# A one-core attention and gated-FFN kernel: stacks moved in halves, even head groups first, the weight comparison on Pool and ScalarE, and unread TensorE passes in the start and in the seam

## The chip, the core and the metric

The kernel runs on one core of a Trainium2 chip. The metric is the device time of one execution in microseconds (us). A core has five engines that run their own instruction streams and wait for each other through semaphores: TensorE (PE; its weight loads are shown apart as PEld), VectorE (DVE), ScalarE (ACT), GpSimd (POOL) and SyncE (SP), which here only issues DMA transfers. ACT issues some transfers too; while it does, it computes nothing.

## The reference

Input x has 32 sequences of 256 tokens with 128 features, in fp32. One layer is computed:

```python
Q, K, V = split_heads(x @ Wq.T + bq), ...          # 16 heads of 8
scores = Q K^T / sqrt(8);  causal mask;  scores -= (i - j)
attn   = softmax(scores);  out = attn V
x = layernorm(x + out @ Wo.T + bo)
h = silu((x @ w1.T) * s1) * ((x @ w2.T) * s2)       # 128 -> 512
h = gelu((h @ h1.T) * sh1);  h = gelu((h @ h2.T) * sh2)   # 512 -> 512
x = layernorm(x + (h @ w3.T) * s3)
```

The FFN weights are small integers times a factor. The kernel looks at run time whether all of them survive a rounding to the matmul's fp32r form without loss; if so, it runs a branch in which each FFN product takes two passes (a rounded part and the rest of the activations), else one with plain fp32. With the inputs here the first branch runs.

## The kernel before

**Pairs.** Two sequences (512 tokens) make a pair; there are 16, numbered n. `project(n)` loads x, turns it over on PE, and makes q and k as 128 x 512 (`pq`, `pk`); ACT adds the bias and rounds (`qhi`, `khi`), DVE takes the rest (`qlo`, `klo`).

**Stacks.** The scores of a head are one matmul of 62 to 64 rows: rounded and rest parts of 8 features, position terms, the mask, and for the second use the maxima. `fill` writes the position rows of the tiles `qs[n % 2]` and `ks[n % 2]` (128 x 8 x 512), and `stack(n, ...)` (L305) moves the q and k parts into them by DMA: for q, and for k, four transfers of 256 KB, 16 target partitions by 8 groups of heads by 512 tokens. A head group g (0 to 7) is one slice of those tiles. q goes on SP's queue; k goes on ACT's queue for pairs 0, 1 and 2 and on SP's later.

**Maxima, then weights.** `row_maxima(n, i)`, i = 0 to 11, computes scores with queries on partitions, in one of three PSUM tiles of two banks (`two`), adds the mask by four small bf16 matmuls (`mask`), and DVE reduces them to maxima (`m`). Of each three, two handle one group each and the third the diagonal blocks of both groups. `maxima_to_rows` turns maxima over on PE (`pm`), ACT copies (`mhi`), DVE takes the rest (`mlo`), and SP moves both into the last rows of `qs`. For pair 0 that is done in two parts, groups 0 to 3 and 4 to 7. `weigh(n, i)` then computes the scores the other way round, with the maxima subtracted in the matmul; ACT takes Exp (`e`), POOL zeroes what the mask hides. `outputs` multiplies by the values (`pa`), and turns the result over (`pt`); `finish` applies Wo (`pon`, `po`).

**Order.** The wrapper `InOrder` keeps PE, DVE, ACT and SP in the order in which the code is written. That order sets all: an engine that waits holds everything behind it. `step(n)` runs the twelve weights of pair n between the twelve maxima of pair n + 1, and between them the projection of pair n + 2 and ends of earlier pairs; then it stacks pair n + 2; then the FFN of pair n - 1 (`feed`) runs with the rest of the attention of pair n (`rest`). Maxima run `LEAD` = 2 places ahead in step 0 and `LAG` = 3 behind in step 1. Step 0 has no FFN, so the way from its last weights through `rest` to step 1 is called the seam. Between step 0 and step 1 each engine reads a number and branches.

**Before step 0** (L684 to L720): projections of pairs 0 and 1 with their fills and stacks, the twelve maxima of pair 0, the load of the FFN layers (2.9 MB, SP), and the first two maxima of pair 1.

**The comparison.** `inexact_weights` (L622) goes through 11 blocks of 128 x 512 weights, one between two score blocks of step 0. ACT rounds a block (`w_near`, `h_near`), DVE compares it with the whole and adds up the differences (`differ`); at the end PE adds over partitions (`pcount`), DVE makes a number of it.

**Waits of transfers.** The built program gives transfers eight completion semaphores in turn, and a transfer waits, on the engine that issues it, until the last one that used its semaphore has landed.

Of the kernel before, what the change touches and what calls it, by code (L numbers as in the profile page):

```python
# [17 lines left out]
P = 128  # L18
# [43 lines left out]
def tile_attn_ffn(  # L62
# [49 lines left out]
    ks = [const.tile([P, W, TOK], F32R, name=f"ks{i}") for i in range(2)]  # L112
    sctx = ctx.enter_context(ExitStack())
# [20 lines left out]

    wq_sb = const.tile([P, D], F32, name="wq_sb")
# [10 lines left out]
    for src, w_bias, bias, nm, eng in (  # L146
        (wqT, bq_sb, bq, "q", act), (wkT, bk_sb, bk, "k", sp),
    ):
        raw = setup.tile([P, D], F32, name=f"raw{nm}")
        eng.dma_start(out=raw, in_=src)  # L150
        raws.append(raw)
        for p in range(2):

            eng.dma_start(
                out=w_bias[64 * p : 64 * p + 64, :],
                in_=bias.rearrange("(f p) d e -> p d e f", p=2)[p],
            )
# [7 lines left out]
    for raw, dst, scale in zip(raws, (wq_sb, wk_sb), (HD**-0.5, 1.0)):  # L165
        act.activation(
            dst.rearrange("i (p d g) -> i p d g", p=2, g=W),
            raw.rearrange("i (g p d) -> i p d g", p=2, g=W), AF.Copy, scale=scale,
        )
    act.activation(bq_sb, bq_sb, AF.Copy, scale=HD**-0.5)  # L170
# [41 lines left out]
    fill(ks[0], "k", act)  # L212

# [13 lines left out]
    for i in range(2):  # L227
# [10 lines left out]
        ("w1", w1T, 1, HID), ("w2", w2T, 1, HID), ("h1", h1T, KC, HID), ("h2", h2T, KC, HID),  # L238
        ("w3", w3T, KC, D),
# [9 lines left out]
    def load_layers(pool):  # L249
        got = {}  # L250
        for nm, src, k, o in layers:
            got[nm] = pool.tile([P, k, o], F32, name=f"{nm}_sb")
            sp.dma_start(out=got[nm], in_=src.rearrange("(k p) o -> p k o", p=P))
        return got
# [40 lines left out]
    def halves(n, ps, bias, nm):  # L295
        pool = setup if n == 1 else hlp
        hi = pool.tile([P, TOK], F32R, name=f"{nm}hi_{n}", tag=f"{nm}hi")
        act.activation(hi, ps, AF.Identity, bias=bias)
        lo = pool.tile([P, TOK], F32R, name=f"{nm}lo_{n}", tag=f"{nm}lo")
        vec.scalar_tensor_tensor(  # L300
            lo, ps, bias, hi.bitcast(F32), ALU.add, ALU.subtract
        )
        return hi, lo

    def stack(n, nm, eng=sp):  # L305
        for r, part in {
            "q": ((0, 0), (1, 0), (2, 1), (3, 1)), "k": ((0, 0), (2, 0), (1, 1), (3, 1))
        }[nm]:
            eng.dma_start(
                out=pairs[n][nm][PAIRING + r :: W, :, :].bitcast(F32),  # L310
                in_=pairs[n][nm + "s"][part].bitcast(F32),
            )
# [309 lines left out]
    def inexact_weights():  # L622

        found = const.tile([P, 11], F32, name="found")
        at = 0
        for nm, *_ in layers:
            rows = [t[nm].rearrange("p k o -> p (k o)") for t in (loaded, near)]
            for c in range(0, rows[0].shape[1], HID):
                whole, part = (t[:, c : c + HID] for t in rows)
                act.copy(part, whole)  # L630
                differ = once.tile([P, HID], F32, name=f"differ_{at}", tag="differ")
                vec.scalar_tensor_tensor(
                    differ, whole, 1.0, part.bitcast(F32), ALU.mult, ALU.not_equal,
                    accum_out=found[:, at : at + 1],
                )
                at += 1
                yield
        ones_col = const.tile([P, 1], F32, name="ones_col")
        nc.gpsimd.memset(ones_col, 1.0)
        count = work("pcount")  # L640
# [41 lines left out]


# [6 lines left out]
    stack(0, "k", act)  # L690
    fill(ks[1], "k", act)
# [3 lines left out]
    run(ahead)  # L695
    stack(1, "q", sp)
    stack(1, "k", act)
    project_values(0)
    for a in range(G):
        act.dma_start(  # L700
            out=wo_sb[C * HD * a : C * HD * (a + 1), :],
            in_=woT[:, :, a, :].rearrange("c d o -> (c d) o"),
        )
    sctx.close()
    ep = enter(tc.tile_pool(name="ep", bufs=5))
    op = enter(tc.tile_pool(name="op", bufs=2))
    yp = enter(tc.tile_pool(name="yp", bufs=2))
    lctx = ctx.enter_context(ExitStack())
    once = lctx.enter_context(tc.tile_pool(name="once", bufs=1))
    for i in range(6):  # L710
        row_maxima(0, i)
    project_values(1)
    maxima_to_rows(0, (0,))
    loaded = load_layers(once)
    for i in range(6, 3 * G):
        row_maxima(0, i)
    maxima_to_rows(0, (1,))
# [7 lines left out]
    def step(n, exact=None, ws=None, hp=None, gp=None):  # L725
# [4 lines left out]
            last(n - 2, exact, ws, gp) if n > 1 else first_norm(0) if n else inexact_weights()  # L730
        )
        ahead = project(n + 2) if n + 2 < NPAIR else iter(())
        for i in range(3 * G):
            weigh(n, i)
            j = i + {0: LEAD, 1: -LAG}.get(n, 0)
# [11 lines left out]
            if i in ((0, 2) if n > 1 else (0, 2, 4, 6)) if n else i < 11:  # L747
                next(settling, None)
# [10 lines left out]
        if n + 2 < NPAIR:  # L759
            stack(n + 2, "q")  # L760
            stack(n + 2, "k", sp if n else act)


        def rest():
            for _ in range(3):
                next(side)
                yield
# [12 lines left out]
            next(last_steps)  # L780
            yield
# [102 lines left out]
```

## Time and profile before

| | us |
|---|---|
| median of three runs (822.67 to 824.28) | 822.67 |
| profiled execution, whole time | 824.84 |
| its span | 822.9 |
| PE busy in the span | 781.9 |
| DVE busy | 635.9 |
| ACT busy | 527.7 |
| POOL busy | 260.6 |

The span is what the profile covers, from the first instruction to the last; all times below count from its start. A busy PE is not PE at its peak: the ends of its pipelined matmuls are modelled, and its clock is granted by a throttle (0.968 of full in the mean here, 1.00 in the body). The busy share is a mean over stages with different limits: 15 steps of the body are alike, and the start, step 0 and the seam are not. In the groups, all instructions of the ordered engines have line 58, that of the wrapper, so they are told apart by their tiles.

### The profile page before, as it was taken

Reading aid. Unit: us, or ns where it says so; the run is one execution under the profiler, and the core shown is the slowest. Engines: PE = TensorE matmul, PEld = TensorE weight load, DVE = VectorE, ACT = ScalarE, POOL = GpSimd, SP = SyncE. Lnnn points to the kernel's source line nnn. Section 1 sums busy time; section 2 is a strip of 40 time slices with the busy share of each in tenths; the row PEclk is TensorE's granted clock in tenths of the full one; section 3 lists DMA queues with packets and bytes.
Section 4 is the critical chain, followed back from the end, with each engine's and each line's share of the span. In section 5 each row is a group of like instructions: output and inputs, shape, how many; then the busy total and the mean of one; then the engine's idle time right before and its main releaser. Section 6 shows DMA issues by size and latency. Waiting matters only on the chain.

```text
span 822.9 us, 17420 instructions
## 1 busy us (share of the span) xinstructions
PE 781.9 (95%) x7046; PEld 554.9 (67%) x7046; DVE 635.9 (77%) x1247; ACT 527.7 (64%) x719; POOL 260.6 (32%) x341
## 2 busy tenths in 40 slices
PE   4897999999999999999999999999999999999995
PEld 1664576676767677676767767676766767666673
DVE  6786777878788887888878887888888788873674
ACT  5055556667676776666576676657666676758673
POOL 5032413323142332414242341424233232424211
PEclk8569999999999999999999999999999999999997
DMA  6824040402304040320404041140404023000001
GB/s 148 209 63 108 14 106 14 105 16 60 73 14 106 27 107 14 81 53 14 106 27 106 14 104 29 36 97 15 107 26 104 4 57 64 14 5 14 0 3 41
DMA packets 39898, 47.49 MB, mean 58 GB/s; under 512 B 3968, under 2 KB 21632, under 8 KB 39808
## 3 DMA queue, kind: packets, MB, share of 16 engines
q1 hardware_dynamic: 37152, 42.82, 21.8%
q10 hardware_dynamic: 2656, 3.48, 1.9%
q8 instruction: 57, 0.93, 0.5%
q14 instruction: 33, 0.27, 0.1%
HBM read 7.48 MB, written 4.19 MB: 14 GB/s over the span
## 4 chain that ended last, share of the span: by engine, by line
PE 80%; ACT 5%; DVE 3%; issue 1%; DMA 1%; SPq 0%; POOL 0%; ACTq 0%; POOLq 0%; DVEq 0%
PE peven L58 14%; PE podd L58 14%; PE pa L58 11%; PE pw L58 10%; PE s L58 10%; PE s_2d L58 2%; PE s_3d L58 2%; PE s_1d L58 2%; PE po L58 2%; ACT e L58 2%; PE pt L58 2%; PE pk L58 2%; PE pv L58 2%; PE s_0d L58 1%; PE pq L58 1%; ACT yT L58 1%
## 5 line engine op out<-in xcount | busy, mean ns | idle before, releaser
L58 DVE TENSOR_REDUCE m<-s 128x4 f32<-128x1024 f32 x128 | 155.6, 1218 | 11.0 <-PE s L58 9.4
L58 ACT ACTIVATE e<-s 128x1024 f32<-128x1024 f32 x128 | 130.6, 1021 | 44.9 <-PE s L58 30.6
L463 POOL TENSOR_SCALAR_AFFINE_SELECT e<-e 128x512 f32<-128x512 f32 x128 | 83.1, 650 | 221.5 <-ACT e L58 192.2
L58 PE MATMUL podd<-h,h_near 128*128 128x512 f32 x512 | 131.4, 403 | 0.9 <-DVE m L58 0.5
L58 PE MATMUL peven<-hodd,h_near 128*128 128x512 f32 x512 | 122.7, 396 | 0.0
L58 PEld LDWEIGHTS peven<-hodd,h_near 128*128 128x128 f32 x512 | 95.7, 187 | 23.4 <-DVE hodd L58 0.3
L58 PEld LDWEIGHTS podd<-h,h_near 128*128 128x128 f32 x512 | 91.7, 188 | 23.1 <-DVE h L58 3.5
L58 ACT ACTIVATE hodd<-podd,sh 128x512 fp32r<-128x512 f32 x64 | 44.1, 688 | 62.8 <-PE podd L58 62.6
L58 PE MATMUL pw<-x1T,w_near 128*128 128x512 f32 x256 | 75.6, 418 | 1.1 <-DVE h0w L58 1.1
L58 PEld LDWEIGHTS s<-qs,ks 64*128 64x128 f32 x512 | 39.1, 189 | 51.9 <-DVE m L58 17.9
L58 PE MATMUL pa<-e,vaug 128*32 128x256 f32 x1024 | 72.2, 397 | 0.0
L274 POOL TENSOR_TENSOR rsa<-rsa,half 128x4 f32<-128x4 f32 x16 | 16.3, 1018 | 175.9 <-DVE rsa L58 175.9
L58 DVE SCALAR_TENSOR_TENSOR h0w<-pw,s,sg 128x512 f32<-128x512 f32 x64 | 47.9, 748 | 30.3 <-ACT sg L58 30.3
L58 PE MATMUL s<-qs,ks 64*128 64x256 f32 x512 | 65.6, 336 | 1.0 <-ACT e L58 0.5
L58 DVE TENSOR_TENSOR heven<-evenw,heven 128x512 fp32r<-128x512 f32 x64 | 44.2, 692 | 26.6 <-ACT evenw L58 26.1
L58 ACT ACT_TABLE_LOAD x47 | 60.3, 1283 | 3.5 <-issue 2.6
L58 ACT ACTIVATE sg<-pw,s 128x512 f32<-128x512 f32 x64 | 43.7, 684 | 28.2 <-PE pw L58 27.8
L58 ACT ACTIVATE heven<-peven,sh 128x512 fp32r<-128x512 f32 x48 | 33.4, 696 | 39.8 <-PE peven L58 39.8
L58 PE MATMUL s<-ks,qs 62*128 62x256 f32 x512 | 55.8, 297 | 2.6 <-ACT e_0d L58 2.1
L58 PEld LDWEIGHTS pw<-x1T,w_near 128*128 128x128 f32 x256 | 43.4, 188 | 18.4 <-ACT nothing L58 5.8
L581 POOL TENSOR_TENSOR h<-h0w,h 128x512 fp32r<-128x512 f32 x31 | 40.0, 1291 | 43.5 <-DVE h L58 41.2
L58 DVE TENSOR_TENSOR hodd<-oddw,hodd 128x512 fp32r<-128x512 f32 x64 | 43.7, 684 | 10.0 <-ACT oddw L58 9.8
(147 smaller groups left out, 1415.7 us busy)
## 6 DMA issues: line engine op xcount, KB each, us to landing
qs<-qhi SPq DMA_DIRECT2D x32, 256.0 KB
qs<-qlo SPq DMA_DIRECT2D x32, 256.0 KB
ks<-khi SPq DMA_DIRECT2D x26, 256.0 KB
ks<-klo SPq DMA_DIRECT2D x26, 256.0 KB
x<-in_x_dram SPq DMA_DIRECT2D x16, 256.0 KB
out_dram<-z SPq DMA_DIRECT2D x15, 256.0 KB
ks<-khi ACTq DMA_DIRECT2D x6, 256.0 KB
ks<-klo ACTq DMA_DIRECT2D x6, 256.0 KB
```

The costliest lines, as they stand in the source:

```text
L58: return lambda *args, **kw: self.tc.keep_in_program_order(call(*args, **kw))
L274: nc.gpsimd.tensor_tensor(rs, rs, half[:, 0:NT], ALU.pow)
L463: nc.gpsimd.affine_select(out=on_diagonal, in_=on_diagonal, pattern=[[0, on_diagonal.shape[1]], [1, P]], base=0, channel_multiplier=-1, co ...
L581: (nc.gpsimd if o < (1 if final else 2) else vec).tensor_tensor(h[:, 1, o, :], whole, h[:, 0, o, :].bitcast(F32), ALU.subtract)
```

## The change

1. `stack` moves each part in two halves: the order of the weights' columns is changed so that 64 source partitions hold the even groups and 64 the odd ones, and the transfers of the even groups come first. 16 transfers of 128 KB take the place of 8 of 256 KB, for each pair. For pairs 1 and 2, k moves from ACT's queue to SP's.
2. Maxima of pair 0 run in the order 0, 3, 6, 9 (even groups), 1, 2, 4, 5, then 7, 8, 10, 11. DVE's `qlo` and `klo` of pair 1 (`due`) come after the first two.
3. The FFN layers are loaded right after the stacks of pair 0, w3 before h1 and h2; the pools that the FFN and outputs use are made earlier, and no longer share memory with the set-up.
4. The comparison runs before step 0: ACT rounds, POOL subtracts, ACT takes the absolute value with a sum, one block behind. The last sum is in place 5 of step 0 and the count in place 8. DVE's part is gone but for one small compare.
5. `warm` issues passes of 512 bf16 columns whose result nobody reads: 4 ahead of the first maxima, 1 behind each of the last four, 4 before the second `maxima_to_rows`, and in `rest` of step 0 four times 4: 28 in all.
6. Smaller: the biases are loaded by SP in one transfer each; the scaling of `bq` is behind the first key fill; Wo is loaded by SP; the value products of pairs 0 and 1 come after the eighth maxima.

```diff
+    lctx = ctx.enter_context(ExitStack())
+    once = lctx.enter_context(tc.tile_pool(name="once", bufs=1))
     sctx = ctx.enter_context(ExitStack())
...
+    for w_bias, bias in ((bq_sb, bq), (bk_sb, bk)):
+        sp.dma_start(out=w_bias, in_=bias.rearrange("c d (e o) -> (c d e) o", o=1))
...
     fill(ks[0], "k", act)
+    act.activation(bq_sb, bq_sb, AF.Copy, scale=HD**-0.5)
...
-        vec.scalar_tensor_tensor(
-            lo, ps, bias, hi.bitcast(F32), ALU.add, ALU.subtract
+        due.append(
+            lambda: vec.scalar_tensor_tensor(lo, ps, bias, hi.bitcast(F32), ALU.add, ALU.subtract)
         )
+        if n != 1:
+            run_due()
...
     def stack(n, nm, eng=sp):
-        for r, part in {
-            "q": ((0, 0), (1, 0), (2, 1), (3, 1)), "k": ((0, 0), (2, 0), (1, 1), (3, 1))
-        }[nm]:
-            eng.dma_start(
-                out=pairs[n][nm][PAIRING + r :: W, :, :].bitcast(F32),
-                in_=pairs[n][nm + "s"][part].bitcast(F32),
-            )
+        for f in range(2):
+            for r, part in {
+                "q": ((0, 0), (1, 0), (2, 1), (3, 1)), "k": ((0, 0), (2, 0), (1, 1), (3, 1))
+            }[nm]:
+                eng.dma_start(
+                    out=pairs[n][nm][PAIRING + r :: W, f::2, :].bitcast(F32),
+                    in_=pairs[n][nm + "s"][part][64 * f : 64 * f + 64, :].bitcast(F32),
+                )
...
     def inexact_weights():
...
+        def add_up(rest, total):
+            act.activation(rest, rest, AF.Abs, accum_out=total)
...
                 act.copy(part, whole)
-                differ = once.tile([P, HID], F32, name=f"differ_{at}", tag="differ")
-                vec.scalar_tensor_tensor(
-                    differ, whole, 1.0, part.bitcast(F32), ALU.mult, ALU.not_equal,
-                    accum_out=found[:, at : at + 1],
-                )
+                nc.gpsimd.tensor_tensor(whole, whole, part.bitcast(F32), ALU.subtract)
+                left.append((whole, found[:, at : at + 1]))
+                if at:
+                    add_up(*left.pop(0))
                 at += 1
                 yield
+        add_up(*left.pop())
+        yield
...
+        vec.tensor_scalar(found, found, 0.0, None, ALU.not_equal)
...
+    def warm(count):
+        t = two("warm")
+        for i in range(count):
+            pe.matmul(
+                t[:, i % 2, :], lhsT=ident_b, rhs=ident_b.unsqueeze(1).to_broadcast([P, NT, P]),
+                start=True, stop=True,
+            )
...
     stack(0, "q", sp)
     stack(0, "k", act)
+    loaded = load_layers(once)
     fill(ks[1], "k", act)
     ahead = project(1)
     next(ahead)
     fill(qs[1], "q", vec)
     run(ahead)
+    warm(4)
+    for i in (0, 3):
+        row_maxima(0, i)
+    run_due()
     stack(1, "q", sp)
-    stack(1, "k", act)
-    project_values(0)
+    stack(1, "k", sp)
+    comparison = inexact_weights()
+    for _ in range(3):
+        next(comparison)
     for a in range(G):
-        act.dma_start(
+        sp.dma_start(
...
-    for i in range(6):
+    for i in (6, 9, 1, 2, 4, 5):
         row_maxima(0, i)
+        if 3 < i < 6:
+            next(comparison)
+    project_values(0)
     project_values(1)
     maxima_to_rows(0, (0,))
-    loaded = load_layers(once)
-    for i in range(6, 3 * G):
+    for i in (7, 8, 10, 11):
         row_maxima(0, i)
+        warm(1)
+        for _ in range(2 if i < 9 else 1):
+            next(comparison)
+    warm(4)
     maxima_to_rows(0, (1,))
...
             weigh(n, i)
+            if n == 0 and i == 5:
+                next(comparison)
+            if n == 0 and i == 8:
+                run(comparison)
...
             stack(n + 2, "q")
-            stack(n + 2, "k", sp if n else act)
+            stack(n + 2, "k")
...
             for _ in range(3):
                 next(side)
+                if n == 0:
+                    warm(4)
                 yield
...
             last_steps = finish(n)
             next(last_steps)
+            if n == 0:
+                warm(4)
             yield
```

## The prediction

> **What bounds the kernel now.** I read the page's first two parts (share of each engine, the forty slices), then the chain that ended last, then busy time by stage, then the timeline from 0 to 90 us. The page gives:
>
> ```profile
> span 822.9 us, 17420 instructions
> PE 781.9 (95%) x7046; PEld 554.9 (67%) x7046; DVE 635.9 (77%) x1247; ACT 527.7 (64%) x719; POOL 260.6 (32%) x341
> ...
> PE   4897999999999999999999999999999999999995
> ...
> PEclk8569999999999999999999999999999999999997
> ```
>
> The chain that ended last opens with PE 80%; ACT 5%; DVE 3%. PE is full from the fifth slice on; only the first four slices (about 82 us) have a lower clock and gaps. By stage (length, then busy time of PE, PEld, DVE, ACT, POOL, then clock, DMA share, GB/s):
>
> ```profile
> 12.00:31.00 19.00, 14.47 (x78) 9.64 (x79) 12.11 (x14) 4.86 (x3) 3.56 (x4) 0.60 1.07 234
> 34.80:44.00 9.20, 6.39 (x54) 4.17 (x54) 7.48 (x8) 0.85 (x2) 0.00 (x0) 0.57 0.93 309
> 43.00:57.00 14.00, 14.00 (x112) 8.85 (x112) 10.83 (x17) 8.10 (x11) 5.33 (x9) 0.51 0.16 41
> 57.00:69.70 12.70, 11.86 (x166) 7.56 (x162) 12.58 (x23) 10.84 (x16) 5.72 (x7) 1.00 0.01 2
> 84.00:87.40 3.40, 3.40 (x28) 1.80 (x26) 2.52 (x4) 0.00 (x0) 1.90 (x5) 0.50 0.26 77
> 132.00:179.40 47.40, 47.15 (x442) 33.93 (x441) 37.81 (x73) 32.25 (x45) 15.68 (x20) 1.00 0.24 58
> ```
>
> A step of the body is 47.35 us (third diagonal score of one step to that of the next, 141.20 to 188.55), PE at 99%, full clock. Step 0's first half runs at half clock, PE full; its second half has DVE at 99%. In the timeline (start, length, instruction, idle before):
>
> ```profile
> 14.98 3.71 ACT L58 ACTIVATE ks<-kconst,col_k_base 128x4096 fp32r<-128x4096 f32 x1 [4.44 <-DVE qs L58]
> 22.11 0.79 PE L58 MATMUL s<-ks,qs 62*128 62x256 f32 x4
> ...
> 42.84 0.80 PE L58 MATMUL s<-qs,ks 64*128 64x256 f32 x4
> ...
> 62.21 0.67 DVE L58 SCALAR_TENSOR_TENSOR differ<-h_sb,h_near 128x512 f32<-128x512 f32 x1
> ...
> 69.78 1.43 ACTq L58 DMA_DIRECT2D ks<-khi  x2
> ...
> 72.41 2.25 SPq L58 DMA_DIRECT2D qs<-qhi  x2
> ...
> 83.39 0.50 PE L58 MATMUL s<-ks,qs 62*128 62x256 f32 x4 [2.12 <-ACT e_0d L58]
> ```
>
> First maxima 22.11, first weights 42.84, seam after 69.7. At 83.39 PE waits for the first maxima of pair 2; the Exp named ended at 82.55, so I read it as the stack of pair 2, whose transfers run until about 81.9.
>
> **The body.** After the branch PE, DVE, ACT and POOL have the same instructions in the same order; only SP changes, 16 stack transfers of 128 KB for 8 of 256 KB in each step. Eight issue in 5.4 us (200.54 to 205.98); sixteen, at the 0.50 of the smallest stack-queue transfers (maxima rows, 16 KB) up to 0.67 each, take 8 to 10.7. Behind them stand the maxima rows:
>
> ```profile
> 200.54 1.24 SPq L58 DMA_DIRECT2D qs<-qhi  x2
> ...
> 204.55 1.43 SPq L58 DMA_DIRECT2D ks<-klo  x2
> 208.69 0.56 SPq L58 DMA_DIRECT2D qs<-mhi  x1
> 211.43 0.56 SPq L58 DMA_DIRECT2D qs<-mlo  x1
> ```
>
> They may be held from 208.69 until 211.2, and are read only by the weights of the next step, some 15 us later (its third diagonal scores are at 235.9); the maxima of the stacked pair come no sooner. Cost 0; without that slack, up to 5 us a step. The Trainium skill, DMA: Bandwidth & Descriptors, "Anatomy of one DMA", gives a fixed 2.0 us a DMA plus bytes at 436 GB/s; taken end to end that estimate is 37 us for the halves against 21, and speaks against them. Here eight transfers overlap, so it isn't in the sum.
>
> **Stage A, to the first weights.** Stacking pair 0 moved 2.1 MB from 11.7 on at about 234 GB/s. Even groups now need half of it: 1.05 MB, until about 16.3, and 1.4 us until the wait opens (81.9 to 83.36 at the seam): first maxima at 17.8 instead of 22.11. That does not carry. The built program lets each transfer wait for an earlier one (eight completion counters in turn; ACT uses four in stacking pair 0), so ACT's last four issues wait for its first four to land: ACT is free at about 18.4 instead of 14.93. Queued behind them are ks fill 3.71, qhi and khi (1.3): 23.4; klo on DVE until 24.3. Only two reductions fit before; six more of 1.22 end at 31.6. The value products at half clock (2.07 each, 29.6 to 33.6, the second partly warm), maxima rows on PE 0.7, copy 0.6: mhi of the first half at 34.4 to 35.0. Behind it on ACT stand six rounds of the comparison: copy 0.61, Abs with sum (not in the trace; between the copy's 0.61 and the 0.70 of an activation with 512 columns, plus 0.1 to 0.3 for the sum, if it is read out as DVE's 0.08 is), beside Pool's subtraction of 1.29 (its 128x512 row in the body, `L581 POOL TENSOR_TENSOR h<-h0w,h`). I take 1.4 a round, ends 1.2 and 1.9: ACT reaches the mhi of the second half at 43.4 (42.2 to 46.4) instead of 41.0. The maxima themselves would be ready sooner: mlo until 35.7, four reductions until 40.6, rows on PE at 41.3. DVE waits there for it, and behind it stand the first reductions of pair 1: 46.0 instead of 43.4. PE's third score block waits for that. The SP queue now carries layers and stacks before the maxima rows: 7.3 MB from 11.7 on (4.2 at 234 GB/s, 3.1 at 309) end near 39.8; the 16 KB rows behind them land about 43, so the first weights are at 43.5, 0.7 late, not the bound. DVE has lost the differ work (0.75 each, two by the fourth block), so by the fourth weight block (49.15 before) I expect 50.0: **+0.85**, ends -1 and +3.5. Moving the bias loads to SP frees ACT's 1.3 us at the start, but the key fill waits for kconst and weights at 5.67 anyway: 0, ends -0.3 and +0.2.
>
> **Stage B, step 0.** Fourth to sixth weight block is 7.84 us at half clock (49.15 to 56.99). At full clock the same pieces are: scores 0.50 and 0.66, maxima 0.92 and 0.72, pa 1.07 and 0.64, pq 1.13, together 5.3 with gaps: 2.5 less. Here the clock decides. It changed at 12.2, 15.7, 19.1, 32.75, 36.15, 56.6, 70.3, 73.7, 84.0 and 87.4, all multiples of about 3.4 us apart; it rose after dense work (projections, pv, pa) and fell with maxima alone (36.15), idle only 0.9 of 3.4. The passes added around the maxima (0.23 each, as body products of 512 columns: 3.73 for 16) fill gaps, but they end before the DVE wait at 43.5 to 46. I take half: **-1.25**, ends 0 and -3.5. The skill, TensorE: Matmul & The Clock Gate, "Part 1: The HAM clock gate", has the same window of 3.4 us and full clock after one busy window; by that alone the sum would have the whole 2.5, but PE was full from 40.9 to 56.6 at half clock here, and the measurement decides. From the sixth block to the last (12.0 us) PE was idle 1.2, waiting for DVE; six differs of 0.75 go: **-1.0**, ends 0 and -1.5. The late part of the comparison is one Abs and a count: 0, up to +0.5.
>
> **Stage C, the seam.** I count from the maxima rows of pair 1 on PE (68.46). SP began stacking q 3.95 later, ACT k already at 69.78. Now k stands behind q on SP, but the first maxima need 12 of 16 pieces: 3.95, 1.2 until bytes flow, 12 of 0.56 to 0.62, 1.4: 13.3 to 13.9, against 14.93: **-1.3**. The odd groups (15.5 to 16.4) are needed about 16.9: hidden. PE's own way to the first weights of pair 1 stays 10.6: 16 passes add 3.7, some 1.8 in gaps, against a warm pa (-1.3) and the count's wait of 1.04, gone. After it 84.0 to 87.4 ran cold, some 1.5; half of it: **-0.7**.
>
> **Sum.** 0.85 - 1.25 - 1.0 - 1.3 - 0.7 = -3.4. The profiled execution took 824.84 (span 822.9, 1.9 around it), 2.2 over the median 822.67; the part that differs is taken off the median: **819.3**.
>
> **Rivals.** (1) The clock stays low in step 0, as it did from 36.15 to 56.6: the passes do not do what they are for. For: the wait at 43.5. Then 1.25 is lost, and the 0.7 perhaps: 820.5 to 821.2. (2) It ends slower: ACT's comparisons. If a round takes 2.2 instead of 1.4, six rounds are 4.8 later, the third block comes near 51, and with a cold step A+B is +5 against -2.3 of relief and seam: 825.4. It decides from about 2.0 a round; Pool's adds at 8.45 took 0.89 instead of 0.43 beside DVE's fills, which speaks for it; DVE now reads PSUM, beside which Pool took 0.45 (46.8), against. (3) Everything stays warm, and ACT gets through sooner: A -0.5, B -3, relief -1.3, seam -2.3: 815.6.
>
> **How the numbers follow.** Forecast 0.42 (817.5 to 820.5), rival 1 0.25, rival 2 0.17, rival 3 0.16. 0.2% is 1.6 us, about what a measurement here tells from no change. Rival 1 is half in the band. Faster 0.69, same 0.15, slower 0.16; the range 815.3 to 824.3 leaves out half of rival 2 and a third of rival 3.
>
> **What would show it.** Right: first maxima near 18, ACT's ks fill after 18, mhi of the second half at 43 with copies and Abs up to it, last score of step 0 by 68, first maxima of pair 2 near 81, body steps of 47.35. Wrong: body steps longer; clock at half through 57; Abs rounds of 2 us; or a stack whose halves fall below 200 GB/s, which would put the rows past 45 and the seam back.

## The result: 0.34% slower

Over nine runs each, the changed kernel took 826.56 us in the median (824.37 to 829.24) and the kernel before 823.91 (822.67 to 824.86): ratio 1.0034, 95% interval 1.0024 to 1.0045. The forecast was 819.3, and its range ended at 824.3. A second comparison, ten runs and 17, gave 825.28 against 823.03, ratio 1.0027 (1.0015 to 1.0038). The ratios here and below are not quotients of two medians; where that matters, the medians are given beside them.

The profiled execution hides this. It is one of the shortest of the changed kernel, 824.37 us, while that of before, 824.84, is one of its longer ones. The page of the changed kernel:

```profile
span 822.6 us, 17689 instructions
PE 784.7 (95%) x7074; PEld 555.3 (67%) x7074; DVE 628.6 (76%) x1226; ACT 536.1 (65%) x743; POOL 273.6 (33%) x352
...
PE   5889999999999999999999999999999999999995
...
PEclk9669999999999999999999999999999999999998
```

PE is full one slice sooner, and the clock of the first two slices is up; in the mean it is 0.975 of full, from 0.968. By stage, in five of the windows shown of before (length, then PE, PEld, DVE, ACT, POOL, clock, DMA share, GB/s):

```profile
34.80:44.00 9.20, 6.88 (x64) 3.68 (x63) 5.36 (x6) 7.76 (x19) 7.49 (x6) 1.00 0.40 131
43.00:57.00 14.00, 11.87 (x82) 7.24 (x82) 8.44 (x8) 4.67 (x5) 4.67 (x9) 0.53 0.11 25
57.00:69.70 12.70, 12.37 (x182) 8.16 (x182) 9.79 (x14) 8.85 (x12) 4.73 (x6) 0.98 0.00 1
84.00:87.40 3.40, 3.40 (x29) 1.92 (x30) 3.40 (x5) 0.07 (x1) 2.97 (x6) 0.63 0.26 83
132.00:179.40 47.40, 47.15 (x443) 33.93 (x442) 37.83 (x73) 32.26 (x45) 15.67 (x20) 1.00 0.18 58
```

The clock is up from 33.6 to 44, where PE is busy for 6.88 of 9.20 us, and falls again for the first half of step 0. DVE is no longer full in the second half. The body is as before. The timeline (start, length, engine and instruction, idle before it) where the forecast had put its marks:

```profile
18.26 0.50 PE L58 MATMUL s<-ks,qs 62*128 62x256 f32 x4 [1.07 <-DMA qs<-qhi]
18.97 3.71 ACT L58 ACTIVATE ks<-kconst,col_k_base 128x4096 fp32r<-128x4096 f32 x1 [8.30 <-DMA ks<-khi]
...
40.83 0.64 SPq L58 DMA_DIRECT2D qs<-mhi  x1
...
43.16 0.58 ACT L58 CAST mhi<-pm 8x512 fp32r<-8x512 f32 x1 [0.62 <-DMA qs<-mhi]
...
43.52 0.50 PE L58 MATMUL s<-qs,ks 64*128 64x256 f32 x4 [1.72 <-DMA qs<-mlo]
43.76 0.68 DVE L58 TENSOR_TENSOR mlo<-pm,mhi 8x512 fp32r<-8x512 f32 x1 [3.84 <-ACT mhi L58]
```

The first maxima came at 18.26, ACT's fill after 18, mhi of the second half at 43.16, first weights at 43.52, all near the forecast. But ACT waited 0.62 us before that mhi for a transfer, though the forecast had it busy with its comparison rounds until then. That small wait was the clue.

### The profile page after: what moved, and what is told of

It reads as the page before. It is cut to its first block, busy times and chain, and to the rows that moved or that the text cites. A ratio compares the mean times of both kernels' runs of the same rounds, so it can differ in the third digit from the quotient of the medians.

```text
span 822.6 us, 17689 instructions
## 1 busy us (share of the span) xinstructions
PE 784.7 (95%) x7074; PEld 555.3 (67%) x7074; DVE 628.6 (76%) x1226; ACT 536.1 (65%) x743; POOL 273.6 (33%) x352
## 4 chain that ended last, share of the span: by engine, by line
PE 84%; ACT 6%; DVE 5%; DMA 2%; SPq 1%; issue 1%; POOL 0%; ACTq 0%; POOLq 0%; DVEq 0%
PE peven L58 14%; PE podd L58 14%; PE pa L58 12%; PE s L58 11%; PE pw L58 10%; PE s_1d L58 2%; PE s_2d L58 2%; PE s_3d L58 2%; PE pv L58 2%; ACT e L58 2%; PE po L58 2%; PE s_0d L58 2%; PE pt L58 2%; PE pk L58 2%; PE pq L58 2%; PE pxT L58 1%
## 5 line engine op out<-in xcount | busy, mean ns | idle before, releaser
L58 PEld LDWEIGHTS podd<-h,h_near 128*128 128x128 f32 x512 | 91.7, 188 | 23.2 <-DVE h L58 3.5
L58 ACT ACTIVATE heven<-peven,sh 128x512 fp32r<-128x512 f32 x48 | 33.4, 696 | 39.8 <-PE peven L58 39.8
L58 PEld LDWEIGHTS pw<-x1T,w_near 128*128 128x128 f32 x256 | 43.4, 188 | 18.4 <-ACT nothing L58 5.8
L595 POOL TENSOR_TENSOR h<-h0w,h 128x512 fp32r<-128x512 f32 x31 | 40.1, 1292 | 43.5 <-DVE h L58 43.5
```

The costliest lines, as they stand in the source:

```text
L58: return lambda *args, **kw: self.tc.keep_in_program_order(call(*args, **kw))
L595: (nc.gpsimd if o < (1 if final else 2) else vec).tensor_tensor(h[:, 1, o, :], whole, h[:, 0, o, :].bitcast(F32), ALU.subtract)
```

## The experiments

The marks in this part are starts on ACT's queue: *mhi 2*, the copy of the second half's maxima of pair 0; *pm 1* and *pm 2*, the copies of the maxima rows of pairs 1 and 2 (PE's transposes stand 0.64 ahead). From pm 1 to pm 2 is called the seam.

| run | median (n) | ratio to before, 95% | mhi 2 | pm 1 | seam |
|---|---|---|---|---|---|
| before | see above | | 40.99 | 69.10 | 48.94 |
| before2 (before once more) | 824.31 (8) | 1.0012 (0.9996, 1.0029) | 41.02 | 69.10 | 48.51 |
| changed | 826.56 (9) | 1.0034 (1.0024, 1.0045) | 43.16 | 70.32 | 48.06 |
| again | 825.28 (10) | 1.0027 (1.0015, 1.0038) | 45.49 | 72.78 | 48.00 |
| nowarm | 826.92 (7) | 1.0053 (1.0035, 1.0071) | 45.31 | 72.97 | 48.68 |
| bodywhole | 826.21 (6) | 1.0043 (1.0031, 1.0056) | 43.52 | 71.22 | 47.17 |
| dvecompare | 827.11 (5) | 1.0060 (1.0047, 1.0073) | 42.86 | 69.82 | 48.01 |
| rowsfirst | 824.15 (11) | 1.0013 (1.0004, 1.0022) | 42.64 | 68.71 | 47.70 |
| rowsfew | 823.33 (11) | 1.0005 (0.9996, 1.0014) | 41.19 | 68.82 | 47.98 |
| rowsfewh2 | 823.54 (11) | 1.0000 (0.9984, 1.0015) | 40.74 | 69.79 | 48.15 |
| whole1 | 827.64 (5) | 1.0063 (1.0049, 1.0077) | 42.35 | 68.31 | 50.04 |
| warmonly | 823.81 (12) | 1.0012 (0.9996, 1.0028) | 44.68 | 69.48 | 48.72 |
| halvesonly | 832.62 (5) | 1.0110 (1.0092, 1.0127) | 43.90 | 72.73 | 54.17 |
| evenfirst | 821.92 (12) | 0.9981 (0.9968, 0.9994) | 40.96 | 68.02 | 47.04 |
| evenfirst2 | 822.66 (12) | 0.9981 (0.9972, 0.9991) | 40.17 | 69.55 | 47.13 |
| evendve | 824.71 (12) | 1.0014 (1.0000, 1.0029) | 39.78 | 67.95 | 48.21 |
| evenwarm | 821.38 (12) | 0.9994 (0.9970, 1.0018) | 39.90 | 66.95 | 47.02 |
| seamonly | 825.77 (12) | 1.0026 (1.0014, 1.0037) | 41.30 | 68.68 | 49.85 |

A profile is one execution and may lie off its median, as the changed kernel's does. Medians of different runs compare only roughly, since the runs of before beside them had medians of 823.03 to 823.91; the ratios allow for that. The kernel of before against itself (before2) shows how far a ratio can lie from 1 without any change.

### First: where the time is

Three theories stood against each other: the start (S), the body's sixteen transfers (B), the unread passes (P).

**again**: no edit.

> The changed kernel once more, for a second profile: the first one comes from an execution of 824.37 us, 2.2 under the median of 826.56. Theory S (the start: ACT's comparison, the SP queue and a cold clock in the first half of step 0 make pair 1's maxima rows late, and how late depends on where the clock changes fall): a profile of an execution near 826.5 shows body steps of 47.35 to 47.37 as before, and the excess of about 2.2 us stands before the first body step: pm of pair 1 later than 69.68, or the first maxima of pair 2 later than 83.50. Theory B (the sixteen stack transfers of a body step hold something now and then): pm at 69.7 and the seam at 83.5 as in the first profile, and some of the 14 body steps longer than 47.4, by 2.2 us in all. Theory P (the unread passes): the seam from pm to the first weights longer by 1 to 2 us.

Its profiled execution took 826.79, near the ordinary. Set against the first profile instruction by instruction, DVE's stream runs 0.6 to 0.7 us ahead until 39, and then there is one place where it falls behind: `mlo` of the second half (43.76 to 46.10), 2.33 us that it keeps, within 0.3 us, to the end. Body steps are the same. SP's queue, then ACT, PE and DVE in the timeline of this run:

```profile
28.31 2.04 SPq L58 DMA_DIRECT2D qs<-qhi  x2
34.13 1.78 SPq L58 DMA_DIRECT2D qs<-qlo  x2
36.01 1.18 SPq L58 DMA_DIRECT2D ks<-khi  x2
...
41.08 2.00 SPq L58 DMA_DIRECT2D wo_sb<-in_woT_dram  x4
43.18 0.64 SPq L58 DMA_DIRECT2D qs<-mhi  x1
```

```profile
45.49 0.57 ACT L58 CAST mhi<-pm 8x512 fp32r<-8x512 f32 x1 [3.69 <-DMA qs<-mhi]
45.88 0.80 PE L58 MATMUL s<-qs,ks 64*128 64x256 f32 x4 [1.79 <-DMA qs<-mlo]
46.10 0.68 DVE L58 TENSOR_TENSOR mlo<-pm,mhi 8x512 fp32r<-8x512 f32 x1 [6.90 <-ACT mhi L58]
```

What SP waited for between 20 and 47 (us in total, times, longest):

```profile
SPq L58 <- DMA h_sb<-in_h2T_dram: 3.8, 1, 3.8
```

From the bottom up: DVE waits 6.90 us for ACT's `mhi`. ACT waits 3.69 us because both halves of the maxima share one buffer (`mhi`, `bufs=1`), and the transfer that reads the first half out of it was issued only at 43.18, though ACT had written those rows by 34.0. On SP it stands behind pair 1's whole stack and `wo`. The stack's seventh piece waited until 34.13 for the landing of the 1 MB layer h2, which had the same completion semaphore; in the first profile until 31.09. From there ten pieces of about 0.6 to 0.9 follow, and four of `wo` of 0.42 to 0.6. I call this theory Q; its rival C says that clock and comparison set the start and the queue only goes along.

**nowarm**: `warm()` issues nothing.

> The changed kernel without a single unread pass (warm() issues nothing). Theory S: the passes are not what costs; without them the clock falls again between 33.6 and 44 and in the seam, as before the change, so no gain: 826 to 827.5 us, granted clock in the profile about 0.970 instead of 0.975. Theory P (they take PE's time, 24 of 0.23 to 0.45 us on the path at the seam, and a score tile each time): 824 to 825 us, first weights of pair 1 before 79.0. Theory B: no change, 826.5.

826.92: P falls. The clock is back at 0.967, pm 1 is as in again, the seam 0.7 longer.

**bodywhole**: pairs 3 to 15 use weights in the old column order and

```diff
+        if n >= 3:
+            for r, part in {
...
+                eng.dma_start(
+                    out=pairs[n][nm][PAIRING + r :: W, :, :].bitcast(F32),
+                    in_=pairs[n][nm + "s"][part].bitcast(F32),
+                )
+            return
```

> The changed kernel, but pairs 3 to 15 are stacked by whole transfers, eight of 256 KB as before the change (their projections use a second copy of the query and key weights in the old order; Pool makes it in the start). Pairs 0 to 2 keep the halves. Theory B: the excess goes, 824 to 824.5 us. Theory S: nothing changes beyond 0.5 us, 826 to 827 us, SP's stacking in the body back to 5.4 us a step instead of 10.3. Theory P: 826.5.

826.21: B falls. The forecast's zero for the body holds. One thing is the experiment's own: from pm 2 to the last maxima rows this kernel takes 609.8 us, where the kernels with one copy of the two weights take 608.9 to 609.1. The other two with a second copy (whole1 and seamonly, below) take 609.8 as well: some 0.75 us more, 0.05 a step. Why is not shown. Without it the median would be about 825.5, still above what B allowed.

**dvecompare**: the comparison of before, beside step 0.

```diff
-                nc.gpsimd.tensor_tensor(whole, whole, part.bitcast(F32), ALU.subtract)
-                left.append((whole, found[:, at : at + 1]))
...
+                vec.scalar_tensor_tensor(
+                    differ, whole, 1.0, part.bitcast(F32), ALU.mult, ALU.not_equal,
+                    accum_out=found[:, at : at + 1],
+                )
...
```

> The changed kernel, but the weights are compared as before the change: copies on ACT and one not-equal with a sum on DVE for each block, beside step 0, instead of a Pool subtraction and an ACT Abs with a sum partly ahead of step 0. Theory S: ACT reaches the maxima rows of the second half 2 us sooner (41 instead of 43.2), the first reductions of pair 1 end near 43.5 instead of 45.6, the first weights stay near 43.3 (the rows' transfers); eleven reads of 0.75 on DVE return to step 0, which then takes 25.6 us from the first weights to pm of pair 1 as before: pm near 68.9 instead of 69.7, 825 to 826 us. Theory B and P: DVE has 8.2 us more in step 0 and nothing else changes, 827 to 829 us.

S expected mhi 2 at 41, since ACT has nothing to do ahead of it. It came at 42.86:

```profile
40.88 0.64 SPq L58 DMA_DIRECT2D qs<-mhi  x1
...
42.86 0.57 ACT L58 CAST mhi<-pm 8x512 fp32r<-8x512 f32 x1 [9.03 <-DMA qs<-mhi]
```

ACT stood idle 9.03 us for the transfer. So it isn't ACT's rounds that hold the start, and the miss of this expectation speaks for Q: the rows on SP's queue alone suffice. The median, 827.11, fits the other theories' 827 to 829 better than S's 825 to 826; its profile, 824.77, is its shortest execution.

### Second: take the rows out of the queue

**rowsfirst**: the first half's rows ahead of the key stack; nothing else.

```diff
-    stack(1, "k", sp)
...
     maxima_to_rows(0, (0,))
+    stack(1, "k", sp)
+    for a in range(G):
+        sp.dma_start(
...
```

The loop is that of the four `wo` loads, which move along.

> The changed kernel with one reordering on SP's queue: the maxima rows of pair 0's first half stand ahead of pair 1's key stack and the output weights, instead of behind them. Theory Q (the queue: the rows land at 43 to 45.5 behind sixteen stack transfers of 0.6 us, one of which waits for the 1 MB layer loads; ACT can't write the second half's mhi before, because both halves share one buffer, and DVE's first reductions of pair 1 stand behind it): mhi of the second half at 42.5, when ACT is through its rounds, instead of 43.16 and 45.49 in the two profiles; first weights near 41 instead of 43.5 and 45.9; reductions of pair 1 from 43; 1 to 3 us less than the changed kernel, 823.5 to 824.5 us. Theory C (the clock and the comparison set the start, the queue only accompanies them): nothing gained, 825.3 to 826.5 us; first weights early, but the third block no sooner than 47.9.

824.15, about half of the loss. From its timeline:

```profile
35.61 0.63 SPq L58 DMA_DIRECT2D qs<-mhi  x1
...
42.64 0.56 ACT L58 CAST mhi<-pm 8x512 fp32r<-8x512 f32 x1
...
44.03 0.69 PE L58 MATMUL s<-ks,qs 62*128 62x256 f32 x4 [1.66 <-DMA ks<-klo]
```

mhi 2 has no wait any more and comes at 42.6, where the rounds end. But the first weights came at 44.90, not at 41: PE now waits 1.66 us for the odd half of pair 1's key stack, issued last. The wait has moved to the next piece in the queue.

**rowsfew**: also four comparison rounds fewer ahead of mhi 2.

```diff
-        for _ in range(2 if i < 9 else 1):
+        for _ in range({7: 1, 8: 1, 10: 0, 11: 0}[i]):
...
-            if n == 0 and i == 5:
+            if n == 0 and i in (0, 1, 2, 3, 5):
```

> As rowsfirst, and four of the six comparison rounds that stand on ACT between the two mhi copies go into step 0, one each after its weight blocks 0 to 3. Theory Q: with the queue out of the way ACT's rounds are what is next (42.5); without four of them, 5.4 us, mhi of the second half comes at 40.6, when the last reduction of pair 0 and its transposes allow it, and pair 1's reductions begin 2 us sooner than in rowsfirst: 821.5 to 823 us. Theory C for the clock: TensorE stays cold anyway and the blocks of step 0 take the same time from the fourth on: 824 to 825 us. If ACT in step 0 can't take the rounds in its gaps (8.1 of 14 us busy there): Exps late, 824 to 826 us.

mhi 2 at 41.19; 823.33, as fast as before and no faster: PE still waits 1.72 us for the same stack half. Less came than Q expected.

**rowsfewh2**: the h2 load behind the key stack.

```diff
-    loaded = load_layers(once)
+    loaded = load_layers(once, layers[:4])
...
     stack(1, "k", sp)
+    loaded.update(load_layers(once, layers[4:]))
```

> As rowsfew, and the second 1 MB layer load (h2) goes behind pair 1's key stack on SP. Theory Q: the seventh piece of pair 1's query stack no longer waits for the landing of h2 (31.1 and 34.1 in the two profiles), the key stack ends near 38 instead of 41 and the first maxima of pair 1 never wait for it; the spread between executions falls under 2 us and the median is 0 to 1 us under rowsfew: 821 to 823 us. Otherwise: as rowsfew.

A miss: 823.54, and the key stack ended at 41.3, not 38. The piece that had waited for h2 now waited 3.6 us for h1. Whichever layer load stands there must land before the semaphore can be used again.

**evenfirst**: rowsfew, and pair 1's maxima also begin with the even groups.

```diff
-    for i in range(LEAD):
+    for i in (0, 3):
         row_maxima(1, i)
...
-                row_maxima(n + 1, j)
+                row_maxima(n + 1, j if n or j > 3 else (0, 3, 1, 2)[j])
```

> As rowsfew, and pair 1's maxima also take the even groups first: blocks 0, 3, 1, 2 instead of 0, 1, 2, 3. In rowsfew PE waits 1.7 us at 42 to 44 for the odd half of pair 1's key stack, with the first weights behind it. Theory Q: that wait goes, the first weights come at 43 instead of 44.6, the reductions of pair 1 follow each other, pm of pair 1 1 to 1.5 us sooner: 821.5 to 822.5 us. Theory C (the clock): 823.3 us as rowsfew.

821.92, ratio 0.9981 (0.9968 to 0.9994): 0.19% faster than before, and faster than the changed kernel. The same engines as above:

```profile
40.96 0.57 ACT L58 CAST mhi<-pm 8x512 fp32r<-8x512 f32 x1 [3.30 <-PE pm L58]
41.56 0.68 DVE L58 TENSOR_TENSOR mlo<-pm,mhi 8x512 fp32r<-8x512 f32 x1 [1.30 <-ACT mhi L58]
...
42.17 3.47 DVE L58 TENSOR_REDUCE m<-s 128x4 f32<-128x1024 f32 x3
42.32 0.50 PE L58 MATMUL s<-qs,ks 64*128 64x256 f32 x4
```

In this profile ACT waits for the maxima and nothing else, and DVE has three reductions in a row. C, which had allowed 825.3 to 826.5, 824 to 825 and 823.3 for rowsfirst, rowsfew and evenfirst, is out as the whole cause; what the clock is worth is taken up below.

**evenfirst2**: evenfirst once more.

> evenfirst again beside the others, for its interval and a second profile. Theory Q: its start does not wait for SP's late pieces any more, so pm of pair 1 stands within 0.5 us of 68.0 and the ratio to before is 0.997 to 0.999.

The ratio came again, 0.9981 (0.9972 to 0.9991). The expected start did not: pm 1 at 69.55 instead of 68.02 with the same program, first weights 43.24 instead of 42.32, and the clock low until 57.5 instead of 55.3. The queue is still in it. PE in this profile:

```profile
42.01 0.50 PE L58 MATMUL s<-ks,qs 62*128 62x256 f32 x4 [1.88 <-DMA ks<-klo]
```

SP had waited 4.0 us for h2, in the first profile 2.3, and pair 1's even key pieces went out 0.9 later; so the first reduction of pair 1 started 0.6 later, although mhi 2 came 0.8 sooner. The rest of the 1.5 comes later, with the clock low in another stretch; how it divides is not shown.

**whole1**: halves for pair 0 alone (as bodywhole, from n = 1).

> The changed kernel with halves only for pair 0; pairs 1 to 15 are stacked by whole transfers, eight of 256 KB, in the same place of SP's queue (a second copy of the two weights in the old order, made by Pool; two more bias loads at the start). Theory Q: SP issues eight transfers of 0.6 us for pair 1 instead of sixteen, and the ring of counters no longer wraps onto the 1 MB loads: the first half's rows are issued near 33 to 35, as soon as they are there, and mhi of the second half comes at 42.5; first weights near 41: 823 to 824.5 us, less whatever the halves gave at the seam (1.1 us, lost again). Theory C: 825.5 to 827 us.

mhi 2 came at 42.35, as Q expected, and pm 1 at 68.31; but SP still waited 2.4 us for h2, and the rows went out at 39.02 instead of 33 to 35, the first weights at 43.07 instead of 41. The seam became 2 us longer, not 1.1. And 827.64 is above all that Q allowed, even with the seam's 2 us added, and 1.9 over its own profiled execution, 825.78. The second copy's 0.75 is part of it; where the ordinary executions of this kernel lose the rest, no profile shows.

### Third: the parts by themselves

**before2**: no edit.

> The kernel before the change once more, for a second profile of it: the first comes from an execution of 824.84 us, 1.5 over the median of all its runs. Theory Q (the changed kernel loses on SP's queue ahead of step 0, which this kernel does not have): the start is the same in every execution here, maxima rows of the first half issued near 32.4, first weights 42.8, pm of pair 1 at 69.1 within 0.5 us; what the executions differ by lies in the cold windows of the seam. If pm of pair 1 moves by 2 us here too, the spread of the start is not the queue's.

pm 1 at 69.10 both times, to the hundredth: the start of before does not vary in these two profiles. That of the changed kernel's two differs by 2.46.

**warmonly**: before, with the unread passes.

> The kernel before the change with the unread passes alone: four ahead of the first maxima, one after each undivided block of pair 0's second half, four ahead of its transposes, and the sixteen of the seam. Theory Q: the clock stays up from 33 to 44 and in the seam (the mean granted clock rises from 0.968 to about 0.975), the start itself waits for DVE and gains little, the seam 0.6 us as between the changed kernel without and with them: 822.3 to 823.2 us. If the passes cost PE's time: 824 to 825 us.

823.81, no difference that can be told (0.9996 to 1.0028). The mean clock is 0.984, and pm 1 is 0.4 later. Two windows of this run:

```profile
28.80:45.60 16.80, 16.41 (x100) 9.25 (x98) 11.83 (x15) 1.15 (x2) 0.00 (x0) 0.50 0.66 201
46.00:57.00 11.00, 10.09 (x135) 6.77 (x132) 11.00 (x17) 8.70 (x12) 6.68 (x9) 1.00 0.15 34
```

Two effects cancel. Four passes ahead of the first maxima moved those from 22.11 to 23.77, the clock was then at half until 45.6, from 33 to 36 too where before had it full, and mhi 2 came 3.7 late. But step 0 ran at full clock and took 23.2 us from the first weights (46.29) to pm 1, where before took 26.3. So a full clock in step 0 was worth some 3 us in this profile, and the passes ahead of it cost as much.

**halvesonly**: before, with the new column order, halves and even groups first; key stacks of pairs 0 to 2 stay on ACT's queue.

> The kernel before the change with the halves alone: the weights and biases in the new order, every stack in sixteen transfers of 128 KB, even groups first, and pair 0's blocks of even groups first; queues, comparison and all else as before (key stacks of pairs 0 to 2 on ACT's queue, maxima rows of the first half ahead of the layers on SP's). Theory Q: halves by themselves cost nothing where the rows don't stand behind them; the first maxima come at 18 to 20 instead of 22.1, ACT issues eight transfers more for each of pairs 0 and 1 (about 5 us each, some of it in its waits), the seam is 1 to 2 us shorter: 821.5 to 823.5 us. If sixteen pieces cost by themselves (issue on ACT ahead of its halves and fills): pm of pair 1 past 70.5 and 824.5 to 827 us.

832.62, worse than all that was expected. The timeline of its seam:

```profile
76.56 2.41 ACTq L58 DMA_DIRECT2D ks<-khi  x2
79.01 1.67 ACTq L58 DMA_DIRECT2D ks<-klo  x2
...
80.78 0.58 ACT L58 COPY oT<-pa 128x512 f32<-128x512 f32 x1 [6.36 <-DMA ks<-khi]
...
81.42 1.11 PE L58 MATMUL pt<-ident,oT 128*128 128x128 f32 x4 [5.14 <-ACT oT L58]
```

Eight transfers in place of four make ACT's queue 7.3 us long (73.4 to 80.7); its output copy `oT` stands behind them and PE behind that. The start loses as well, 3.6 us at pm 1: with eight pieces of pair 0 to issue, ACT begins its fill at 18.00 instead of 14.98, and the first maxima come at 25.12 instead of 22.11. So halves in the seam need SP's queue; that the change gave pair 1's key stack to SP as well is what then held the rows.

**seamonly**: before up to pm 1; from pair 2 on halves, both stacks on SP, and the passes of the seam.

> The kernel before the change with the change's seam alone: pairs 0 and 1 stacked whole, in the queues and order of before; from pair 2 on halves, query and key both on SP's queue (a second copy of the two weights in the new order, made by Pool), and the sixteen unread passes of the seam. Theory Q: the start stays at 69.1 to pm of pair 1; from its copy to that of pair 2 48.0 instead of 48.9 and 47.6 to 48.5: 0.5 to 0.9 us less than before, 822.5 to 823 us. If the seam's 1 us in the changed kernel came only from the late start of the step ahead of it (pm later, all else waiting for the same transfers): 823.3 us, no gain.

825.77, slower; pm 1 at 68.68, the seam 49.85. The first maxima of pair 2 come 14.47 after pm on PE (14.93 and 14.50 before, 13.82 in the changed kernel), and from 82.2 on the clock is low for 6.8 us, in the changed kernel for 3.4 from 84.9. Of the loss 0.75 is the second copy's in the body. The changed seam is no gain by itself.

**evendve**: evenfirst with the comparison of before.

> As evenfirst (rows ahead of the key stack, even groups first for pair 1 too), but the comparison as before the change: eleven copies on ACT and eleven reads of 0.75 us on DVE beside step 0, no Pool subtraction, no Abs. If DVE's relief is worth the 1.0 us that the prediction gave it or more: 1 to 3 us over evenfirst, pm of pair 1 at 69 to 71. If step 0 is bounded by TensorE at half clock and by the waits ahead of it: within 0.5 us of evenfirst, pm of pair 1 near 68.2.

824.71, and 0.33% between the ratios is 2.7 us; against evenfirst2, run beside it, the medians differ by 2.05. pm 1 is the same as in evenfirst, 67.95; the seam is 1.1 longer. PE in its timeline, at the count:

```profile
69.55 0.17 PE L58 MATMUL pcount<-found,ones_col 128*1 128x11 f32 x1 [1.04 <-DVE mlo L58]
```

The last two reads stand ahead of DVE's `mlo` of pair 1 (67.2 to 68.8), and PE waits 1.04 us for the count; evenfirst counts at 63. So the move of the comparison is a gain. How much of it is DVE's relief is not shown, since ACT's and POOL's part of the comparison changes with it; nor is the place: dvecompare lost as much against again (0.33%, 1.8 us by the medians) with a seam of 48.01, no longer than the changed kernel's.

**evenwarm**: evenfirst, and

```diff
             weigh(n, i)
+            if n == 0 and i < 4:
+                warm(3)
```

> As evenfirst, with three unread passes more after each of the first four weight blocks of step 0, where PE waits for DVE and the clock falls (at 45 in evenfirst, until 55.4). If passes there keep TensorE at full clock: the blocks from the fourth to the sixth take 5 instead of 7 us, pm of pair 1 at 65.5 to 67, 819 to 820.5 us. If the clock falls all the same, or the score tile that each group of passes takes holds the next scores up: pm at 68 to 70, 822 to 824 us.

The windows from 43 to 57, first of evenfirst, then of this run:

```profile
43.00:57.00 14.00, 13.12 (x118) 8.32 (x118) 8.51 (x9) 10.18 (x18) 10.02 (x13) 0.63 0.12 27
```

```profile
43.00:57.00 14.00, 13.36 (x136) 7.34 (x135) 9.03 (x10) 11.05 (x20) 10.19 (x13) 1.00 0.12 27
```

Full clock throughout, and pm 1 at 66.95. Eight of the 12 runs took 820.5 to 821.6, four 824.1 to 829.3. So the ratio is not settled, 0.9994 (0.9970 to 1.0018), though the medians are 821.38 against 823.79; what the four do no profile shows. pm 1 is 1.1 us ahead of evenfirst's 68.02 and 2.6 ahead of evenfirst2's 69.55.

## Why the prediction was wrong

**Stage A: the step that failed.** The **+0.85** failed in two terms. The first is a relief that bought nothing. The forecast let pair 1's first reduction end 2.6 late (46.0 for 43.4) and then had most of that regained by the fourth weight block, since DVE "has lost the differ work (0.75 each, two by the fourth block)". In the first profile the reduction ended a little sooner than forecast, near 45.6, and the block was late all the same. The third block of maxima, which waits for that reduction, and the fourth weight block on PE, first of before, then of the changed kernel:

```profile
43.46 1.12 PE L58 MATMUL s_0d<-ks,qs 62*128 62x128 f32 x8
49.15 0.80 PE L58 MATMUL s<-qs,ks 64*128 64x256 f32 x4
```

```profile
45.63 1.11 PE L58 MATMUL s_0d<-ks,qs 62*128 62x128 f32 x8 [1.60 <-DVE m L58]
51.31 0.80 PE L58 MATMUL s<-qs,ks 64*128 64x256 f32 x4
```

From one to the other it is 5.69 us before and 5.68 after, with PE at half clock and without a gap in both. The forecast's own row of before had PE busy for 14.00 of 14.00 us there, so DVE was not the bound.

The second term is the rows on SP's queue, of which it said that they "land about 43, so the first weights are at 43.5, 0.7 late, not the bound", with the queue's end worked out from bytes and rate, 39.8. In the shorter execution they were issued at 40.83, the weights came at 43.52, and the queue cost ACT no more than its 0.62 us; that this agrees with the forecast is luck, for in again they were issued at 43.18 and the weights came at 45.88. What was wrong is the kind of limit: from 36 to 41 (again) the queue issues a piece of 128 KB every 0.63 us, some 208 GB/s, and ahead of that it stands still until a layer lands on the semaphore. The prediction had used just this rule of semaphores for ACT, where it gave 18.4 for the fill (measured 18.97), and not for SP. And what waits for the rows is not only PE but, because of the one buffer, the next `mhi`, and with it DVE and pair 1's reductions.

Measured at the fourth Exp: 49.98 before, 52.15 and 54.49 in the two profiles, so +2.2 and +4.5 for the **+0.85**; the second is beyond the range's +3.5. Rows ahead of the key stack (rowsfirst) gave 0.14 to 0.21% back, 1.2 to 1.7 us; with four rounds moved and pair 1's even groups first as well (evenfirst) the kernel is faster than before.

**Stage B.** From the fourth Exp to the twelfth it took 19.78 before, 18.83 and 18.94 after: -0.9 for the **-1.25** and **-1.0** together. The clock stayed low from 44 to 57.6, so rival 1 was right about step 0: the passes end before the wait, and in it the clock falls. That passes inside step 0 hold it is shown by evenwarm, in evenfirst's order. The move of the comparison is worth more than 1.0 in the medians of evendve and dvecompare, but the profiles don't show it in step 0.

**Stage C.** First maxima 13.82 and 13.80 after pm instead of 14.93: -1.1 for the **-1.3**; in the second profile of before it is 14.50. But the seam as a whole is only 0.5 to 0.9 shorter, of the 2.0 with the **-0.7** for the cold window, which did not go: 84.9 to 88.3 is cold. nowarm gives the passes 0.65 of it, and seamonly shows that without the rest the halves bring no gain.

**The body.** 47.36 a step instead of 47.35, rows held until 211.66 instead of 208.69, nothing waits: zero was right, and bodywhole agrees. The fixed 2.0 us a DMA that the prediction cites from the Trainium skill is fitted there for transfers that GpSimd issues. These are issued by SP, and no run here tests that figure.

**The rivals.** Rival 2 named the right chain (ACT's mhi, DVE behind it, pair 1's reductions, step 0 cold) with the wrong cause: the six rounds took ACT from 34.59 to 42.54, 1.33 us each, near the 1.4 taken and not 2.2, and without any rounds (dvecompare) mhi 2 came only 0.3 us sooner. Its 825.4 came nearest, by luck.

**The base.** The sum was made against one profiled execution of before that lies 0.9 to 1.8 over the medians of later runs, and its outcome was read in one of the changed kernel that lies 2.2 under. These two differ by -0.3 in span: +1.2 to pm 1, -0.9 in the seam, and -0.6 after it. Second profiles, 824.57 and 826.79, differ by 2.3: +3.68 to pm 1, -0.5 in the seam, +0.1 in the body, -0.95 after the last maxima rows, where the last store's landing varies.

## What to carry to other kernels

Where many small transfers go to one queue, count its issues, its waits for semaphores that come round, and what is queued behind them, not bytes by rate; then ask of each late transfer not only who reads what it brings, but who wants the buffer that it empties. Cutting a transfer in two brought the first maxima sooner here (18.26 for 22.11), but neither run with the halves but without the rest of the change (halvesonly, seamonly) was faster than before; so look first at what stands behind the pieces. Give the small transfer that a whole chain waits for the place ahead, and read the halves in the order in which they come. Before a relief is put into a sum, ask whether the relieved engine is the one that the stage waits for. A profile of one execution may hide a loss that most executions have; take a second one before the traces are compared.

## What the runs showed of the hardware

The issue of a stack piece on SP took 0.6 us whether it moved 128 or 256 KB, where nothing held it (in the body 1.24 us for two pieces, at 200.54 in before with 256 KB and at 200.66 in the changed kernel with 128). Two windows (the last two numbers are the share of the transfer engines' time and GB/s), first of again, pieces of 128 KB, then of whole1 in the seam, 256 KB:

```profile
36.00:41.00 5.00, 3.90 (x33) 1.90 (x34) 3.20 (x3) 4.78 (x12) 4.77 (x4) 1.00 0.62 209
```

```profile
73.00:77.00 4.00, 3.72 (x26) 2.59 (x25) 2.33 (x8) 0.00 (x0) 0.00 (x0) 1.00 1.04 239
```

With whole transfers the engines are full; with halves they stand at 0.62 and the issuing sets the pace. The Trainium skill, DMA: Bandwidth & Descriptors, "Issuing engines are not separate DMA queues", says that issuing from several engines saves only the time to initiate transfers, usually small against the transfers themselves. In this stage it was not small.

With the same program, step 0's cold stretch ran from 45.1 to 55.3 in one execution (evenfirst) and from 43.8 to 57.5 in another (evenfirst2), each change a multiple of some 3.41 us from the last, and pm 1 moved by 1.5, of which 0.6 stood already at pair 1's first reduction. The Trainium skill, TensorE: Matmul & The Clock Gate, "Part 1: The HAM clock gate", calls this window free-running and its effect different from run to run; these two profiles agree.

ACT's absolute value with a sum is two instructions: 0.63 us for 128 x 512, and 0.19 for reading the sum out.
